# A subtraction of the causal convolution moved from VectorE to GpSimd, in the first and the last batch element

## The chip, the core and the metric

The kernel runs on one core of a Trainium2 chip. The core has a matrix engine (TensorE, PE in the profile), a vector engine (VectorE, DVE), a scalar engine (ScalarE, ACT), a general engine (GpSimd, POOL) and a queue engine that issues most of the loads (SyncE, SP). They work side by side and wait for each other on semaphores. The metric is the time of one execution on the device in microseconds (us); lower is better.

## What is computed

The input `x` is (4, 512, 128, 64): four batch elements `b`, T = 512 time steps, and D = 128*64 = 8192 features. Two layers follow one another. The part that matters here is in layer 0, after the attention and the convolution over frequency:

```python
x = x + fo                                            # called x2 in the kernel
xn = layernorm(x.reshape(b, t, d), ln_time_g, ln_time_b)
xt = jnp.swapaxes(xn, 1, 2)
to = lax.conv_general_dilated(xt, time_W, (1,), [(KS - 1, 0)],
                              dimension_numbers=('NCH', 'OIH', 'NCH'), feature_group_count=d)
to = to + time_b[None, :, None]
to = layernorm(jnp.swapaxes(to, 1, 2), time_ln_g, time_ln_b)
x = x + to.reshape(b, t, f, h)
mid = jax.nn.gelu(x @ ffn_W1 + ffn_b1)
x = x + (mid @ ffn_W2 + ffn_b2)
```

The layernorm takes, for each batch element and time step, the mean and the variance over all 8192 features. The convolution has three taps along time, a set of its own for every feature (`KS` = 3), and looks only back. Layer 1 then adds a moving average over time to a filter in the frequency domain (Fourier transform, a matrix product per frequency and channel, inverse transform).

## The kernel before

Layer 0 holds its data with features on the 128 partitions and time along the row. D is cut into `NCH` = 64 chunks of 128 features, and the chunks are handled in `NPR` = 32 pairs; a tile of a pair is 128 partitions x 2 x 512 float32, which the profile writes as 128x1024. For each batch element there are six stages, written as Python generators: `project` and `scan` (attention's projections and its recurrence), `attend_and_convolve` (the attention's output, the frequency convolution, and `x2`, stored to DRAM), `convolve_time` (the causal convolution), `open_feed` and `feed_forward`. A planner, `in_turn`, interleaves two stages at a time, by shares written out by hand. The pairs of stages around the change are `convolve_time(0)` beside `attend_and_convolve(1)`, and `convolve_time(3)` beside `feed_forward(2)`. What the planner sets by hand is TensorE's order alone; the order on the other engines is made by the language's scheduler when the kernel is built, except where an instruction is told to keep the order of the program.

`convolve_time(b)` makes the causal convolution of all 32 pairs. For b = 1 and b = 2, 14 of the 32 (`AHEAD`) are made earlier, in `convolve_ahead`, which runs inside the `feed_forward` of the element before; for b = 0 and b = 3 (`B - 1`) all 32 are made in `convolve_time`. For each pair, `normed` loads `x2` from DRAM on the SP queue (L643), multiplies it by 1/std (`rb`, L644), and subtracts mean/std (`mb`, L647). `rb` and `mb` are rows over time, the same on all partitions, and are read for both chunks of the pair (`pair_of`). All inputs and outputs of L644 and L647 are in SBUF, as float32, and L647 works in place.

`tapped` then makes the convolution, for each of the two chunks: ScalarE multiplies by the last tap and adds the bias (L652), and VectorE adds the other two taps, each a multiply and an add on a shifted row (L656). GpSimd then corrects the first two time steps of both chunks (L662, 128x4 elements) and issues the store of the result (L663). ScalarE makes the square of the result (L703), and TensorE sums the result and its square over the features two steps later (`add_up`, L252), for the second layernorm.

For b = 0 the normed tile has two buffers (`kd`) and the result three (`k3`, named `to`); for b = 3 they are three (`x1`, named `x`) and four (`z`).

In the loop beside `convolve_time(0)`, VectorE also makes, for each pair of b = 1: the sum of attention's output and `x` (L542, its first input in PSUM), its product with 1/std (L546, both inputs in SBUF), and `x2` (L596, its first input in PSUM). GpSimd issues the store of that `x2` (L599). Beside `convolve_time(3)`, VectorE makes, for each pair of b = 2: a product and a difference for the second layernorm (L724 and L725, SBUF), a sum (L736, SBUF), and the two sums that end the feed-forward (L793, first input in PSUM). GpSimd issues the store of every second pair's output (L810).

Only `normed` is edited; it is called from `convolve_ahead` and `convolve_time`.

Of the kernel before, what the change touches and what calls it, by code (L numbers as in the profile page):

```python
# [12 lines left out]
ALU = mybir.AluOpType  # L13
# [67 lines left out]
def layer0(ctx, tc, dram, x, xt, vecs, wkvr, wo, wdec, wconv, fbias, w1, fb1, w2, fb2, x4):  # L81
# [4 lines left out]
    nc = tc.nc  # L86
    B = x.shape[0]
# [202 lines left out]
    def pair_of(row):  # L290
        return row.unsqueeze(1).to_broadcast([P, 2, SL])
# [349 lines left out]
    def normed(b, i, x2, xr, rb, mb, pinned=False):  # L641

        nc.sync.dma_start(x2, x2d[b][2 * i : 2 * i + 2].rearrange("c p t -> p c t"))  # L643
        first = nc.vector.tensor_tensor(xr, x2, pair_of(rb), ALU.mult)  # L644
        if pinned:
            tc.keep_in_program_order(first)
        nc.vector.tensor_tensor(xr, xr, pair_of(mb), ALU.subtract)  # L647

    def tapped(b, i, xr, to, pinned=False):
        for j in range(2):  # L650
# [14 lines left out]
    def convolve_ahead(b, bank):  # L665


        rb, mb = yield from rows(bank, *carried[b], "rm3")
        ahead[b] = rb, mb
        for i in range(AHEAD):  # L670
            xr = spare("x1", SL)
            normed(b, i, xr, xr, rb, mb, True)
            yield
            tapped(b, i, xr, spare("z", SL), True)
            yield

    def convolve_time(b):
# [10 lines left out]
        for k in range(n + 2):  # L688
            while waiting and waiting[0][0] == k - 2:
                add_up(st, 0, *waiting.pop(0)[1:], added == 0, added == NPR - 1)  # L690
                added += 1
            if k < n:
                if b == B - 1:

                    x2, xr, to, sq = spare("xp", SL), spare("x1", SL), spare("z", SL), two(bk, "sq")
                else:
                    x2 = bk.tile([P, 2, SL], F32, tag="kx", name="x2", bufs=3)
                    xr, to = two(bk, "kd"), bk.tile([P, 2, SL], F32, tag="k3", name="to", bufs=3)
                    sq = bk.tile([P, 2, SL], F32, tag="sq4", name="sq4", bufs=2)

                normed(b, made + k, x2, xr, rb, mb, made > 0 and k < 4)
                tapped(b, made + k, xr, to)
                nc.scalar.activation(sq, to, AF.Square)  # L703
                waiting.append((k, to, sq))
                i = k * made // n
                if i != (k + 1) * made // n:

                    to = fetch("kh", tod, b, i)
                    sq = bk.tile([P, 2, SL], F32, tag="mid", name="sq5", bufs=4)
                    nc.scalar.activation(sq, to, AF.Square)  # L710
                    waiting.append((k, to, sq))
            yield 7.0 * (NPR + 2) / (n + 2)
# [532 lines left out]
```

## Time and profile before

| what | value |
|---|---|
| median of 3 runs | 3669.21 us (3665.94 to 3675.53) |
| the profiled execution | 3668.25 us, of which the span of the profile is 3666.5 us |
| clock granted to TensorE, mean over the span | 0.985 |
| L644 and L647 for b = 0 | 32 each, 520 to 767 us from the span's start |
| L644 and L647 for b = 3 | 32 each, 2086 to 2355 us |
| VectorE: L644, L647 | 1.22 us each, 128x1024 |
| VectorE: L656 | 0.74 us each, 128x511 or 128x510 |
| GpSimd: L662 | 128x4, from 0.19 to 8.04 us |

A row of the profile has the line of the kernel, the engine, the operation, the tiles (output<-inputs), the shapes, how often it runs, its busy time and the mean of one. Neighbouring VectorE operations overlap by a few hundredths of a microsecond in the records, so the distance between their starts is a little less than the duration that is shown. The waits view has one line for each pair of a waiting line and the line that it waited for: the sum in us, how many times, and the longest. A duration on GpSimd includes the time in which the operation has been started and waits for SBUF.

### The profile page before, as it was taken

Reading aid. Unit: us, or ns where it says so; the run is one execution under the profiler, and the core shown is the slowest. Engines: PE = TensorE matmul, PEld = TensorE weight load, DVE = VectorE, ACT = ScalarE, POOL = GpSimd, SP = SyncE. Lnnn points to the kernel's source line nnn. Section 1 sums busy time; section 2 is a strip of 40 time slices with the busy share of each in tenths; the row PEclk is TensorE's granted clock in tenths of the full one; section 3 lists DMA queues with packets and bytes.
Section 4 is the critical chain, followed back from the end, with each engine's and each line's share of the span. In section 5 each row is a group of like instructions: output and inputs, shape, how many; then the busy total and the mean of one; then the engine's idle time right before and its main releaser. Section 6 shows DMA issues by size and latency. Waiting matters only on the chain. (4 is left out here: it accounts for less than half of the span.)

```text
span 3666.5 us, 53980 instructions
## 1 busy us (share of the span) xinstructions
PE 3458.3 (94%) x20297; PEld 1363.8 (37%) x20297; DVE 2707.6 (74%) x3530; ACT 1787.3 (49%) x2363; POOL 448.6 (12%) x657
## 2 busy tenths in 40 slices
PE   8989998889998899999899989999999999999998
PEld 3433332234333223433322333343334833328433
DVE  4476779976776996677699799956677277892677
ACT  0013445655666565666656688878864200252100
POOL 0000012210111211010122121100001000001000
PEclk9999999999999999999999999999999999999999
DMA  9876657787885788788478678646668478994688
GB/s 314 288 260 232 225 187 257 257 280 269 288 275 174 265 275 289 271 282 282 164 264 284 214 255 266 227 169 213 233 197 266 149 254 289 300 302 148 224 281 263
DMA packets 427732, 910.48 MB, mean 248 GB/s; under 512 B 32848, under 2 KB 83664, under 8 KB 423376
## 3 DMA queue, kind: packets, MB, share of 16 engines
q1 hardware_dynamic: 353904, 637.11, 53.3%
q0 software_dynamic: 71680, 268.46, 20.3%
q8 instruction: 162, 2.65, 0.3%
q10 hardware_dynamic: 1888, 1.45, 0.1%
q14 instruction: 98, 0.80, 0.1%
HBM read 638.39 MB, written 268.50 MB: 247 GB/s over the span
## 5 line engine op out<-in xcount | busy, mean ns | idle before, releaser
L780 PE MATMUL p<-mid,w_sb 64*64 64x512 f32 x2048 | 551.5, 596 | 17.6 <-DVE wx L793 17.6
L780 PE MATMUL pb<-mid,w_sb 64*64 64x512 f32 x2048 | 534.0, 596 | 0.0
L770 ACT ACTIVATE mid<-c,fb_sb 128x1024 f32<-128x1024 f32 x256 | 284.3, 1111 | 93.0 <-PE c L765 90.8
L770 ACT ACTIVATE mid<-m,fb_sb 128x1024 f32<-128x1024 f32 x256 | 284.6, 1112 | 92.0 <-PE m L765 90.8
L765 PE MATMUL c<-x,w_sb 64*64 64x512 f32 x2016 | 279.0, 606 | 12.8 <-ACT mid L770 6.5
L765 PE MATMUL m<-x,w_sb 64*64 64x512 f32 x2016 | 283.0, 613 | 7.4 <-ACT ob L814 5.0
L780 PEld LDWEIGHTS p<-mid,w_sb 64*64 64x64 f32 x2048 | 154.1, 134 | 291.9 <-issue 262.1
L1091 ACT COPY two<-a 128x512 f32<-128x512 f32 x64 | 37.5, 585 | 432.0 <-PE a L1086 432.0
L414 PE MATMUL a<-xp,wx 128*128 128x512 f32 x512 | 235.2, 603 | 0.5 <-DVE me L269 0.5
L1114 PE MATMUL b<-xin,avg_sb 128*128 128x512 f32 x512 | 230.8, 593 | 3.3 <-DVE xin L1120 3.3
L1120 DVE TENSOR_TENSOR xin<-b,pm 128x512 f32<-128x512 f32 x256 | 159.1, 683 | 101.3 <-PE b L1117 86.3
L601 ACT ACTIVATE sq<-x 128x1024 f32<-128x1024 f32 x128 | 135.0, 1055 | 156.9 <-DVE x L596 156.8
L252 PE MATMUL st<-x,ones 128*32 128x512 f32 x512 | 185.2, 611 | 24.5 <-DVE x L596 24.5
L656 DVE SCALAR_TENSOR_TENSOR to<-kd,vec,to 128x511 f32<-128x511 f32 (+1 forms) x272 | 196.9, 742 | 10.4 <-ACT to L652 8.1
L733 ACT ACTIVATE kd<-kd,vec 128x512 f32<-128x512 f32 x256 | 192.7, 803 | 3.1 <-DVE kd L725 3.1
L966 DVE COPY xf<-b 128x256 f32<-128x256 f32 x128 | 54.3, 424 | 179.0 <-PE b L1060 170.0
L542 DVE TENSOR_TENSOR x<-a,xp 128x1024 f32<-128x1024 f32 x128 | 156.0, 1219 | 38.2 <-PE a L538 35.6
L656 DVE SCALAR_TENSOR_TENSOR z<-x,vec,z 128x511 f32<-128x511 f32 x240 | 175.6, 744 | 5.0 <-ACT z L652 3.6
L736 DVE TENSOR_TENSOR x<-kd,kx 128x1024 f32<-128x1024 f32 x126 | 154.0, 1222 | 33.4 <-ACT kd L733 33.4
L538 PE MATMUL a<-rst,wo_sb 64*64 64x512 f32 x1024 | 143.3, 627 | 27.5 <-DVE x L542 25.2
L793 DVE SCALAR_TENSOR_TENSOR x4t<-p,fb_sb,x 128x512 f32<-128x512 f32 x64 | 47.7, 746 | 160.0 <-PE pb L780 157.6
L724 DVE TENSOR_TENSOR kd<-kh,rm 128x1024 f32<-128x1024 f32 x128 | 155.6, 1219 | 7.1 <-ACT rm L286 4.6
(275 smaller groups left out, 6773.5 us busy)
## 6 DMA issues: line engine op xcount, KB each, us to landing
xp<-in_xt SPq DMA_DIRECT2D x256, 512.0 KB
kh<-to SPq DMA_DIRECT2D x156, 512.0 KB
x<-x POOLq DMA_DIRECT2D x128, 512.0 KB, 4.4
kx<-x SPq DMA_DIRECT2D x128, 512.0 KB
x<-ob POOLq DMA_DIRECT2D x64, 1024.0 KB, 8.1
xin<-x SPq DMA_DIRECT2D x64, 1024.0 KB
out<-xin POOLq DMA_DIRECT2D x64, 1024.0 KB, 6.3
x<-x SPq DMA_DIRECT2D x96, 512.0 KB
```

Source lines behind the costliest of these rows:

```text
L252: nc.tensor.matmul(st[32 * q : 32 * q + 32, :], lhsT=ones, rhs=src[:, j, :], start=first, stop=last,)
L414: nc.tensor.matmul(pa[:, k, :], lhsT=wq[:, j, k * P : (k + 1) * P], rhs=xp[:, j, :], start=first and j == 0, stop=last and j == 1,)
L542: nc.vector.tensor_tensor(x1, at, xp, ALU.add)
L656: tap = nc.vector.scalar_tensor_tensor(to[:, j, k:], xr[:, j, : SL - k], vec[:, w, c], to[:, j, k:], ALU.mult, ALU.add)
L724: nc.vector.tensor_tensor(d, to, pair_of(rb), ALU.mult)
L733: tc.keep_in_program_order(nc.scalar.activation(d[:, j, :], d[:, j, :], AF.Identity, bias=vec[:, B4, c], scale=vec[:, G4, c]))
L736: nc.vector.tensor_tensor(x3, d, x2, ALU.add)
L765: nc.tensor.matmul(pm[halves[j], h, :], lhsT=w1_sb[halves[h], q * H : (q + 1) * H], rhs=x3[halves[h], j, :], start=True, stop=True,)
L770: gelu = nc.scalar.activation(mid, pm, AF.Gelu_apprx_tanh, bias=fb1_sb[:, q : q + 1])
L780: nc.tensor.matmul(sums2[i][j][halves[h], :], lhsT=w2_sb[halves[j], q, :], rhs=mid[halves[j], h, :], start=q == 0, stop=q == 3,)
L1114: nc.tensor.matmul(po[j], lhsT=avg_sb[:, j, :], rhs=xin[:, j, :], start=True, stop=False)
L1120: nc.vector.tensor_tensor(by_n(xin[:, j, :]), by_n(po[j]), by_c(pm[j % 2][:, j // 2, :]), ALU.add)
```

## The change

One line of `normed` changes. The subtraction of mean/std is issued on GpSimd where `b` is 0 or 3; for b = 1 and b = 2 it stays on VectorE. The product with 1/std before it and the taps after it stay where they were.

```diff
         first = nc.vector.tensor_tensor(xr, x2, pair_of(rb), ALU.mult)
         if pinned:
             tc.keep_in_program_order(first)
-        nc.vector.tensor_tensor(xr, xr, pair_of(mb), ALU.subtract)
+        (nc.gpsimd if b in (0, B - 1) else nc.vector).tensor_tensor(xr, xr, pair_of(mb), ALU.subtract)
```

So 64 instructions, 32 in each of the two loops, go from VectorE's queue to GpSimd's. When the kernel is built, the scheduler also orders the other instructions of these two loops on VectorE, ScalarE and SP somewhat differently, since it places the moved instructions anew; TensorE's order stays as it was, and so do the shapes and the number of all instructions and transfers.

## The prediction

> **What bounds the kernel now.** I read the page's busy line first, then the windows around the two loops that the change touches (for batch elements 0 and 3, `b` = 0 and `b` = 3), then the groups and waits inside them. Over the whole span the bound is TensorE:
>
> ```profile
> PE 3458.3 (94%) x20297; PEld 1363.8 (37%) x20297; DVE 2707.6 (74%) x3530; ACT 1787.3 (49%) x2363; POOL 448.6 (12%) x657
> ```
>
> That is an average. In the windows view (PE, PEld, DVE, ACT, POOL busy us, then clock, DMA share, GB/s) the two loops look different:
>
> ```profile
> 508.00:766.00 258.00, 230.86 (x1310) 62.74 (x1309) 251.65 (x274) 154.80 (x212) 68.35 (x91) 0.99 0.76 256
> 2124.00:2355.00 231.00, 211.53 (x1740) 78.35 (x1733) 228.89 (x258) 199.28 (x237) 45.50 (x62) 0.97 0.77 256
> ```
>
> In the first, the causal convolution of b=0 beside attend_and_convolve of b=1, VectorE is busy 251.7 of 258 us. In the second, the convolution of b=3 beside feed_forward of b=2, 228.9 of 231. VectorE sets the pace there, and the waits from 400 to 1000 us and from 2000 to 2450 us agree that TensorE is the one that waits:
>
> ```profile
> PEld st L252 <- DVE x L596: 43.3, 29, 4.6
> PEld a L538 <- DVE x L542: 30.5, 24, 2.2
> PEld p L780 <- DVE wx L793: 25.5, 13, 6.5
> ```
>
> So one microsecond saved or lost on VectorE in these loops is about one microsecond of the kernel, until TensorE binds.
>
> **What is removed.** 32 subtractions (L647) leave VectorE in each loop. One shows as 1.22 us, but three in a row take 3.50 us, so the pitch is (3.50-1.22)/2 = 1.14 us, as neighbours overlap by 0.08. Five taps (L656) in a row take 3.39 us: pitch (3.39-0.74)/4 = 0.66. Removed: 32 x 1.14 = 36.5 us in each loop, 73 us in all. If nothing came back, TensorE's own busy time would stop the gain first: 258-231 = 27 us in the first loop. In the second, 2092 to 2355 us, TensorE is busy 22.7 + 211.5 = 234 of 263 us, so 29. The most that can be won is 56 us.
>
> **What is added.** 64 subtractions on GpSimd, on 128x1024 elements with two SBUF inputs. No row has this, so I bound one from below and above. Of the nearest rows, clearing 128x128 takes 209 ns against 102 for 128x4: 0.86 ns an element. The one-input operation takes 405 ns for 256 elements (L1053) against 228 for 4 (L233): 0.70 an element, though it reads and writes. So one pass costs about 0.8 ns an element, on 0.2 us of fixed time (the 4-element L662 has a minimum of 0.19). With both reads and the write overlapped: 0.2+0.8 = 1.0 us. Reads in turn: 0.2+1.6 = 1.85. All three in turn: 2.65. The two-input 4-element row is too short to choose. I take 2.25, midway between the last two, as I expect the reads not to overlap and do not know of the write.
>
> **What it collides with.** Here is the part that decides. These are lines of the timeline (start, length):
>
> ```profile
> 598.88 1.22 DVE L644 TENSOR_TENSOR kd<-x,rm 128x1024 f32<-128x1024 f32 x1
> 599.11 1.05 POOL L662 TENSOR_TENSOR to<-to,vec 128x4 f32<-128x4 f32 x1 [0.20 <-issue]
> 600.02 1.22 DVE L596 TENSOR_TENSOR x<-c,x 128x1024 f32<-128x1024 f32 x1
> ...
> 608.33 1.22 DVE L596 TENSOR_TENSOR x<-m,x 128x1024 f32<-128x1024 f32 x1
> 608.56 0.19 POOL L662 TENSOR_TENSOR to<-to,vec 128x4 f32<-128x4 f32 x1 [5.40 <-issue]
> ...
> 2107.79 8.04 POOL L662 TENSOR_TENSOR z<-z,vec 128x4 f32<-128x4 f32 x1 [0.23 <-DVE z L656]
> ```
>
> The same four-element GpSimd operation takes 0.19 us beside L596, whose first input is in PSUM, and 1.05 us beside L644, which has both inputs in SBUF: it ends 0.06 us after L644 does (598.88+1.22 = 600.10, and 599.11+1.05 = 600.16). At 2107.79 it waits 8 us, through eight such VectorE operations back to back, and ends as L793, with a PSUM input, starts. The two engines do not read SBUF side by side when VectorE reads two tensors there. What a long GpSimd read does to VectorE, no row shows: four elements are over too soon. From below VectorE loses nothing, from above it stands for all of GpSimd's time that its own PSUM operations do not cover. I take the upper end, since a port that cannot be shared in one direction is unlikely to be shared in the other.
>
> [...]
>
> **The sum.** The built order gives what VectorE issues next after each L644, and GpSimd's L647 waits for that L644. With L644's end as zero: GpSimd begins at 0.145 (as L662 does after a tap), and ends at 0.145 + H. VectorE's next operation starts at -0.08.
> - First loop, 30 of 32 tiles: next is L596 or L542 (PSUM, 1.14), which runs undisturbed. The operation after it should start at 1.06 and starts when GpSimd ends: loss H + 0.145 - 1.06 = H - 0.92. Against 1.14 saved: H - 2.06, which is +0.19 at 2.25.
> - Second loop, 21 of 32: next are two L793 (PSUM, 2 x 0.66): loss H + 0.145 - 1.24, net H - 2.24, which is +0.01.
> - The other 2 and 11: next is L644, L724, L725 or L656, two SBUF inputs, no cover: net H + 0.145 + 0.08 - 1.14 = H - 0.92, which is +1.33.
>
> First loop 30 x 0.19 + 2 x 1.33 = 8.4 us; second 21 x 0.01 + 11 x 1.33 = 14.8; 23 us in all. With H of 1.85 the same sum is -4.4 + 3.3 = -1; with 2.65 it is 21.2 + 27.6 = +49.
>
> The queue behind the new instruction: on GpSimd come the store of x2 (L599, 0.73 us to issue), the fix of the first two steps (L662), the store of its result (L663, 0.72) and in the second loop the store of x4 (L810). Per tile that is 2.25 + 0.73 + up to 1.05 + 0.72 and about a microsecond of waits, some 6 us, against 258/32 = 8.1 us for a tile, so the queue keeps up and stands ready at each L644. Who waits for it: ScalarE's square (L703, now 17.8 us for L662 in all), then TensorE's sums two steps later; a delay of 2 us is inside these two steps. TensorE's order is the same. SP's loads in both loops are issued in a somewhat altered order, with the same transfers; I cost this at nothing, as the windows show a DMA share of 0.76 and no row of VectorE waits for a load there. If that cover went, one load late by its own issue of 0.4 us in each of 64 tiles would be 26 us. What is not covered is the opening of each loop, where taps wait for a first tile: 1.3 us longer in the first, and three in line in the second, some 3 x 1.1 = 3.3 us, less what VectorE does meanwhile. I add 2 us. Total +25 us.
>
> The profiled execution took 3668.25 us (span 3666.5 and 1.75 around it); 3668.25 + 25 = 3693. The median of the three runs is 3669.21, 1 us above, so I leave it at 3693.
>
> **The rivals.**
> 1. VectorE is truly relieved: GpSimd and VectorE alternate at a finer grain, or VectorE's operations go on during GpSimd's. For it: four-element operations delay no VectorE operation visibly. Against: the 8 us wait. Then TensorE binds, at best 3668 - 56 = 3612; as engines in turn wait for each other some half of it is likelier, about 3635. Faster. It decides if VectorE pays less than about 0.9 us for one GpSimd subtraction.
> 2. It comes out even: H near 1.85, so the loss equals what is saved: 3667.
> 3. GpSimd is starved, as at 2107.79, whenever it misses the PSUM operation. The 11 uncovered tiles of the second loop would each finish about 6 us late, and if the taps wait for that, 11 x 6 = 66 us: 3734. Against it: three xr buffers let taps run two tiles behind.
>
> **How the numbers follow.** Forecast 0.53, rival 1 0.24, rival 2 0.18, rival 3 0.05. 0.3% of 3669 is 11 us, about what a measurement of this kernel tells from no change. So slower 0.58, same 0.18, faster 0.24. The low end must take in half of rival 1: 3636. The high end is H = 2.65: 3668 + 49 + 2 = 3719, say 3720. Since cases of both signs carry weight: the forecast's own range is 3680 to 3720.
>
> **What would show it.** Right: L647 on POOL at 2.2 us or more; L656 or L736 stretched from 0.74 and 1.22 us when it follows the PSUM operation, VectorE still busy over 95% in both loops, the first loop longer by some 8 us and the second by 15. Wrong: L656 at 0.74 us throughout and VectorE at about 85%, with the loops shorter; or L647 below 1.9 us. If the loops keep their length but the kernel moves, the reordered loads did it.

## The result, and the profile after

The changed kernel takes 3686.88 us (median of 8 runs, 3678.25 to 3700.57) against 3666.57 us (8 runs, 3659.32 to 3677.37) before: a ratio of 1.0055, 95% interval 1.0042 to 1.0069. It is slower by 0.42 to 0.69%, some 20 us. The profiled execution has a span of 3695.1 us, 28.6 more than the one of before; it is one of the slower ones of its eight.

First the busy line of the changed kernel's page:

```profile
PE 3459.8 (94%) x20297; PEld 1370.5 (37%) x20297; DVE 2710.6 (73%) x3466; ACT 1788.5 (48%) x2363; POOL 605.1 (16%) x721
```

VectorE (DVE) runs 64 instructions fewer and is busy 2710.6 us, 3 us more than before. So the time that the 64 subtractions took is still on VectorE, in other rows. GpSimd (POOL) is busy 156 us longer. The rows of two single lines of code, the subtraction and the taps, show where VectorE's time went (columns: shortest, median and longest in ns, first and last start):

```profile
L647 POOL TENSOR_TENSOR kd<-kd,rm x32: 2347/2360/3322, 524.7 to 777.1; 128x1024 f32<-128x1024 f32 x32
L647 POOL TENSOR_TENSOR x<-x,rm x32: 2345/2363/3349, 2115.2 to 2385.3; 128x1024 f32<-128x1024 f32 x32
```

```profile
L656 DVE SCALAR_TENSOR_TENSOR to<-kd,vec,to x272: 733/744/3276, 528.9 to 2051.2; 128x511 f32<-128x511 f32 x123, 128x510 f32<-128x510 f32 x13
L656 DVE SCALAR_TENSOR_TENSOR z<-x,vec,z x240: 683/743/4271, 889.3 to 2409.9; 128x511 f32<-128x511 f32 x111, 128x510 f32<-128x510 f32 x9
```

The rows of the taps before:

```profile
L656 DVE SCALAR_TENSOR_TENSOR to<-kd,vec,to x272: 729/742/753, 527.1 to 2028.9; 128x511 f32<-128x511 f32 x119, 128x510 f32<-128x510 f32 x17
L656 DVE SCALAR_TENSOR_TENSOR z<-x,vec,z x240: 676/744/790, 871.7 to 2380.5; 128x511 f32<-128x511 f32 x112, 128x510 f32<-128x510 f32 x8
```

The subtraction takes 2.36 us on GpSimd. The taps (L656) have the same median as before, 0.74 us, but the longest went from 0.79 to 4.27. One period of the first loop in the timeline of VectorE, and of GpSimd, shows how (start, length):

```profile
669.38 1.23 DVE L644 TENSOR_TENSOR kd<-x,rm 128x1024 f32<-128x1024 f32 x1
670.52 1.22 DVE L596 TENSOR_TENSOR x<-m,x 128x1024 f32<-128x1024 f32 x1
671.66 2.73 DVE L656 SCALAR_TENSOR_TENSOR to<-kd,vec,to 128x511 f32<-128x511 f32 x2
674.31 1.22 DVE L542 TENSOR_TENSOR x<-a,xp 128x1024 f32<-128x1024 f32 x1
...
678.01 1.23 DVE L644 TENSOR_TENSOR kd<-x,rm 128x1024 f32<-128x1024 f32 x1
```

```profile
670.70 2.36 POOL L647 TENSOR_TENSOR kd<-kd,rm 128x1024 f32<-128x1024 f32 x1
```

A period of the same loop before, on VectorE:

```profile
749.38 1.22 DVE L644 TENSOR_TENSOR kd<-x,rm 128x1024 f32<-128x1024 f32 x1
750.64 1.22 DVE L647 TENSOR_TENSOR kd<-kd,rm 128x1024 f32<-128x1024 f32 x1
751.79 1.22 DVE L596 TENSOR_TENSOR x<-m,x 128x1024 f32<-128x1024 f32 x1
...
756.50 1.53 DVE L656 SCALAR_TENSOR_TENSOR to<-kd,vec,to 128x511 f32<-128x511 f32 x2
758.07 1.23 DVE L644 TENSOR_TENSOR kd<-x,rm 128x1024 f32<-128x1024 f32 x1
```

L596, with an input in PSUM, keeps its 1.22 us under GpSimd's operation. The first of the two taps after it starts at 671.66 and ends only after GpSimd has, which is at 673.06: the pair takes 2.73 us where two taps took 1.40 to 1.53 before. One period is 678.01 - 669.38 = 8.63 us; before, the L644 at 749.38 and 758.07 were 8.69 apart. In the middle of the loop the change is nearly even: 1.2 to 1.3 us of stall in place of 1.14 of subtraction.

I take as stretch what an operation on VectorE lasts beyond the median of its form while L647 runs on GpSimd. It sums to 37.8 us in the first loop and 34.7 in the second, with a median per tile of 1.21 and 1.07 us. The 32 subtractions that were taken away are worth 36.5 us in each loop. So the stalls eat what the relief gives, and little more.

The two windows that follow lie between the same two matmuls of each loop, before and then after (columns as in the windows of the prediction, VectorE the third busy time):

```profile
504.70:809.40 304.70, 271.18 (x1510) 78.91 (x1506) 281.46 (x324) 174.69 (x238) 75.82 (x102) 0.99 0.77 260
2069.90:2385.20 315.30, 280.07 (x2254) 107.41 (x2249) 300.04 (x340) 260.79 (x308) 67.85 (x80) 0.95 0.72 242
```

```profile
505.50:826.90 321.40, 265.76 (x1510) 83.69 (x1506) 285.72 (x292) 175.16 (x238) 155.30 (x134) 0.96 0.75 246
2092.20:2414.70 322.50, 284.74 (x2254) 108.23 (x2249) 297.77 (x308) 261.28 (x308) 146.69 (x112) 0.94 0.72 237
```

Both together are 23.9 us longer. VectorE is busy 2.0 us longer in them and idle 21.9 us longer. So with the stalls set against the relief, the loss in this trace is time in which VectorE has nothing to run.

Where that is, TensorE shows. Its order is the same in both kernels, so the start of the same matmul can be compared. How much later it starts after the change:

```
place (us, trace of before)   504.7   549.5   747.9   809.4   2069.9   2121.9   2187.6   2385.2   end
late by (us)                    0.8     7.5    12.1    17.5     22.3     32.1     28.1     29.5    28.6
```

Of the first loop's 16.7 us, 6.7 come in its opening, 4.6 in the 200 us of its middle, and 5.4 at its end. The second loop loses 9.8 in its opening, wins 4.0 back and loses 1.4 more. Between the loops, where the instructions are the same, the traces drift by 4.8; I do not count that to the change, since the kernel with only the first loop changed (below) drifts by -0.7 there. The opening of the second loop on VectorE and on GpSimd:

```profile
2112.51 1.22 DVE L644 TENSOR_TENSOR x<-xp,rm 128x1024 f32<-128x1024 f32 x1
2118.42 8.03 DVE L656 SCALAR_TENSOR_TENSOR z<-x,vec,z 128x511 f32<-128x511 f32 x7 [4.69 <-ACT z L652]
...
2134.40 3.48 DVE L644 TENSOR_TENSOR x<-xp,rm 128x1024 f32<-128x1024 f32 x3
2142.22 6.25 DVE L656 SCALAR_TENSOR_TENSOR z<-x,vec,z 128x511 f32<-128x511 f32 x4 [4.34 <-ACT z L652]
```

```profile
2115.17 7.42 POOL L647 TENSOR_TENSOR x<-x,rm 128x1024 f32<-128x1024 f32 x3 [10.73 <-ACT rm L286]
...
2133.31 4.63 POOL L662 TENSOR_TENSOR z<-z,vec 128x4 f32<-128x4 f32 x1 [1.36 <-DVE z L656]
2138.24 0.72 POOL L663 DMA_DIRECT2D to<-z  x1 [0.30 <-POOL z L662]
2138.99 6.95 POOL L647 TENSOR_TENSOR x<-x,rm 128x1024 f32<-128x1024 f32 x3
```

Three subtractions stand in a row on GpSimd, 7 us, where VectorE did three in 3.5. VectorE has nothing else to do and is idle for 4.69 and 4.34 us, until ScalarE (L652) has the first tile; before, it was idle here once, for 1.40 us. Then the taps collide with the next subtraction. The second three also start late: the first of the three L644 ends at 2135.62, but the four-element L662 stands ahead in GpSimd's queue and takes 4.63 us beside VectorE's taps and L644, and then the store L663 is issued. So the first subtraction begins at 2138.99, 3.4 us after its input was there.

### The profile page after: what moved, and what is told of

Read it like the earlier page. It is cut to its first block, busy times and chain, and to the rows that moved or that the text cites. A ratio compares the mean times of both kernels' runs of the same rounds, so it can differ in the third digit from the quotient of the medians.

```text
span 3695.1 us, 53995 instructions
## 1 busy us (share of the span) xinstructions
PE 3459.8 (94%) x20297; PEld 1370.5 (37%) x20297; DVE 2710.6 (73%) x3466; ACT 1788.5 (48%) x2363; POOL 605.1 (16%) x721
## 3 DMA queue, kind: packets, MB, share of 16 engines
q8 instruction: 162, 2.65, 0.3%
## 5 line engine op out<-in xcount | busy, mean ns | idle before, releaser
L656 DVE SCALAR_TENSOR_TENSOR to<-kd,vec,to 128x511 f32<-128x511 f32 (+1 forms) x272 | 233.7, 873 | 18.0 <-ACT to L652 13.2
L656 DVE SCALAR_TENSOR_TENSOR z<-x,vec,z 128x511 f32<-128x511 f32 (+1 forms) x240 | 190.3, 806 | 14.1 <-ACT z L652 12.6
L736 DVE TENSOR_TENSOR x<-kd,kx 128x1024 f32<-128x1024 f32 x126 | 171.7, 1363 | 35.0 <-ACT kd L733 35.0
L252 PE MATMUL st<-x,ones 128*32 128x512 f32 x512 | 169.2, 608 | 17.5 <-DVE x L596 17.5
L599 POOL DMA_DIRECT2D x<-x x128 | 93.5, 730 | 483.4 <-DVE x L596 459.2
L793 DVE SCALAR_TENSOR_TENSOR x4t<-p,fb_sb,x 128x512 f32<-128x512 f32 x64 | 47.7, 745 | 159.5 <-PE pb L780 157.0
```

Source lines behind the costliest of these rows:

```text
L252: nc.tensor.matmul(st[32 * q : 32 * q + 32, :], lhsT=ones, rhs=src[:, j, :], start=first, stop=last,)
L656: tap = nc.vector.scalar_tensor_tensor(to[:, j, k:], xr[:, j, : SL - k], vec[:, w, c], to[:, j, k:], ALU.mult, ALU.add)
L736: nc.vector.tensor_tensor(x3, d, x2, ALU.add)
```

## The experiments

All are edits of the one line of `normed`, in the kernel before (one run adds a tile besides). A `+` line stands in place of that line, and `(...)` in it stands for the arguments of the subtraction as it was. Differences in us are worked out from the ratio and 3670 us. TensorE's order is the same in all of them. Theory A: VectorE's operations with two SBUF inputs stand still while GpSimd reads SBUF. Theory B: GpSimd is only a slow link of the chain and a full queue. What is given as "loop I" and "loop II" is how much later the same matmul starts over 504.7 to 809.4 us, or over 2069.9 to 2385.2, in the one trace of that kernel against the one of before (for a loop that a run leaves as it was, it came to 3.5 and 0.0).

**The subtraction left out**

```diff
-nc.vector.tensor_tensor(xr, xr, pair_of(mb), ALU.subtract)
+b in (0, B - 1) or nc.vector.tensor_tensor(xr, xr, pair_of(mb), ALU.subtract)
```

> The subtraction of mean/std is left out for b = 0 and b = 3 (the result of these two lacks it); b = 1 and b = 2 keep it on VectorE. It shows how much VectorE's relief is worth with nothing put in its place. Both theories: faster than before. VectorE loses 2 x 36.5 us; TensorE's own busy time allows 56 us at most; I expect about half to three quarters, 3668 - 30 to 40 = 3628 to 3638. If it is less than 10 us faster, VectorE did not set the pace of the loops, and the theory of the prediction falls at its first step.

Measured: 3623.49 against 3674.86 us, ratio 0.9871 (0.9850 to 0.9891), 47 us less; loop I -31, loop II -15. So VectorE does set the pace, and its relief alone is worth close to the 56 us that TensorE's busy time allowed, more than I expected.

**GpSimd writes, but reads nothing**

```diff
+[nc.gpsimd.memset(xr, v) for v in (1.0, 0.5)] if b in (0, B - 1) else nc.vector.tensor_tensor(...)
```

> In place of the subtraction for b = 0 and b = 3, GpSimd fills the same tile with a constant, twice (the result of these two is not the reference's). This occupies GpSimd for about 2 us at the same place of the same chain, but it reads nothing from SBUF. Theory A (VectorE stands still for the reads of GpSimd): no stretched L656 and L736, loops as short as with the subtraction left out, within 12 us of that run. Theory B (what costs is that GpSimd is a slow link of the chain, in time and in its queue): as slow as the changed kernel, 3680 to 3690.

Measured: 3627.10 against 3674.86, ratio 0.9876 (0.9848 to 0.9903), the same as with the subtraction left out; loop I -25, loop II -21. The rows of this kernel's L647 and L656:

```profile
L647 POOL MEMSET kd<- x64: 946/952/974, 515.1 to 731.1; 128x1024 f32 x64
```

```profile
L656 DVE SCALAR_TENSOR_TENSOR to<-kd,vec,to x272: 732/744/753, 518.9 to 1998.5; 128x511 f32<-128x511 f32 x121, 128x510 f32<-128x510 f32 x15
```

Two fills are 1.9 us at the same place of the same chain. No tap is stretched (longest 0.753 us here and 0.787 in the second loop's row, where it was 0.790 before), and no fill waits (0.942 to 0.978 in both loops). Theory B would have had this kernel at 3680 to 3690; it falls. An occupied GpSimd costs nothing here. Its reads do. For the openings the run says less: the fills do not read mean/std, so they need not wait for that row (L286) as the first subtractions do, and two of them are 0.4 us shorter than one subtraction.

**GpSimd's subtraction added, nothing taken away**

```diff
+free_s, scrap = [True], rowp.tile([P, 2, SL], mybir.dt.bfloat16, tag="scrap", name="scrap")
...
 nc.vector.tensor_tensor(xr, xr, pair_of(mb), ALU.subtract)
+b in (0, B - 1) and nc.gpsimd.tensor_tensor(scrap, xr, pair_of(mb), ALU.subtract)
```

> VectorE keeps all its subtractions, and GpSimd makes the same subtraction once more for b = 0 and b = 3, into a tile that nobody reads (bfloat16, for space). So GpSimd's reads are added and nothing is taken from VectorE or put on the chain. Theory A: each of the 64 costs VectorE 1.2 to 2.3 us, depending on what stands after it in VectorE's queue; 75 to 130 us slower than before, 3745 to 3800. Theory B: nobody waits for the result, so under 12 us slower, 3667 to 3680.

Measured: 3760.29 against 3674.86, ratio 1.0242 (1.0215 to 1.0269), 89 us more; loop I +48, loop II +42. Nobody waits for the result, so theory B does not explain it: 89 / 64 = 1.4 us a subtraction. The stretch on VectorE adds up to 46.4 and 43.5 us, with a median per tile of 1.26 and 1.07, as in the changed kernel. The sum, 89.9 us, is all that the kernel lost. The rows of the added subtraction:

```profile
L647 POOL TENSOR_TENSOR scrap<-kd,rm x32: 2342/2376/3280, 526.7 to 813.5; 128x1024 bf16<-128x1024 f32 x32
L647 POOL TENSOR_TENSOR scrap<-x,rm x32: 2338/2358/3274, 2143.1 to 2447.1; 128x1024 bf16<-128x1024 f32 x32
```

**The first three pairs stay on VectorE**

```diff
+(nc.gpsimd if b in (0, B - 1) and i > 2 else nc.vector).tensor_tensor(xr, xr, pair_of(mb), ALU.subtract)
```

> As the change, but the first three pairs of each loop keep the subtraction on VectorE. In the profile of the changed kernel TensorE falls behind by 6 us in the opening of the first loop and by 10 in that of the second, and by little in between. If the opening carries the loss (pairs in a row with nothing to cover them, and taps that wait): 10 to 15 us less than the changed kernel, 3672 to 3677. If the loss is even over the tiles: 58/64 of it, within 3 us of the changed kernel, 3684 to 3687.

Measured: 3683.15 against 3674.86, ratio 1.0028 (1.0015 to 1.0040), between the two expectations. Loop I +10.6 (16.7 with the change), loop II +3.5 (7.2). In the trace the opening of the first loop is repaired (0.2 us late at 549.5, not 7.5), and that of the second is not: it still loses 6.1 us between 2069.9 and 2121.9. There L662 again takes 4.63 us (at 2117.52), three subtractions follow in a row (at 2123.19, 6.95 us), and VectorE is again idle for 4.34. Loss is left in the first loop after the opening, so the opening carries part of it, not all.

**One loop at a time**

```diff
+(nc.gpsimd if b == 0 else nc.vector).tensor_tensor(xr, xr, pair_of(mb), ALU.subtract)
```

> Only the first loop's subtraction (b = 0) goes to GpSimd. The prediction gave it 8.4 us of tiles and 1.3 of the opening, so 3676 to 3680; the changed kernel's trace has TensorE 17.5 us late after this loop, of which some 5 came at its end while TensorE's clock was halved. If that is part of the change and not chance, 12 to 18 us slower than before; if it is chance, 6 to 12.

```diff
+(nc.gpsimd if b == B - 1 else nc.vector).tensor_tensor(xr, xr, pair_of(mb), ALU.subtract)
```

> Only the second loop's subtraction (b = 3) goes to GpSimd. The prediction gave it 14.8 us of tiles and up to 3.3 of the opening; in the changed kernel's trace TensorE loses 10 us in its opening, wins 4 back, and nothing after. So by the trace 5 to 9 us slower than before, by the prediction 15 to 18. If the two loops do not influence each other, this and the run with b = 0 alone add to the change's 20 us, within 6.

Measured against 3673.50: 3686.26 for b = 0, ratio 1.0036 (1.0023 to 1.0048), and 3679.42 for b = 3, ratio 1.0016 (1.0002 to 1.0029). Together 0.52%, where the change has 0.55: the two loops add. The first costs 13 us, more than the 9.7 that I had given it, and the second 6, less than 15 to 18. By what I had written down, 13 us speaks for the end of the first loop as a part of the change (12 to 18) and not as chance (6 to 12). But it lies close to the bound, and the interval, 0.23 to 0.48%, is 8 to 18 us. In the trace of b = 0 alone the matmuls are again 7.6 us late in the opening; at the end of the loop the lateness grows by 1.7 us, not by 5.4. In that of b = 3 alone, whose first loop is as before, it grows there by 2.6. So I take most of the 5.4 for chance; it is not shown.

**GpSimd takes one chunk of the pair, or a third of the time steps**

```diff
+[e.tensor_tensor(xr[:, j, :], xr[:, j, :], mb, ALU.subtract) for e, j in ((nc.gpsimd, 1), (nc.vector, 0))]
+    if b in (0, B - 1) and i > 2 else nc.vector.tensor_tensor(xr, xr, pair_of(mb), ALU.subtract)
```

> GpSimd subtracts one chunk of each pair (128x512), VectorE the other; the first three pairs of each loop stay on VectorE. If GpSimd's reads are free while VectorE works on a PSUM input, the operation, about 0.2 + 1.08 = 1.28 us long, nearly fits into L596 (1.14) and into the two L793 (1.32): VectorE saves 0.54 us a tile, stands 0.2 in the first loop and 0 in the second, and pays 0.7 more than it saves at the 14 tiles without cover: 26 x -0.34, 18 x -0.54, 14 x 0.7, together -9 us, 3658 to 3668. If cover is of no importance and only the length of GpSimd's operation counts: half of the run with the opening left on VectorE, 3 to 8 us slower than before.

```diff
+[e.tensor_tensor(xr[:, :, s], xr[:, :, s], pair_of(mb)[:, :, s], ALU.subtract)
+    for e, s in ((nc.gpsimd, slice(0, 170)), (nc.vector, slice(170, SL)))] if b in (0, B - 1) and i > 2 else ...
```

> As the run with one chunk, but GpSimd takes the first 170 of 512 time steps of both chunks (128x340), VectorE the rest. The operation should be 0.2 + 0.72 = 0.9 us and fit wholly into the PSUM operations: 0.35 us saved a tile, nothing lost at 44 tiles, 0.45 lost at 14: -9 us, about as the half. If cover is of no importance: no gain, within 5 us of before.

Measured against 3673.50: half 3661.19, ratio 0.9971 (0.9961 to 0.9982), 11 us faster than before; third 3667.19, ratio 0.9980 (0.9967 to 0.9992), 7 us. Both beat the kernel before; between the two there is no certain difference. It is the same engine, the same operation and the same place, but cut to the length of its cover, and with the openings left to VectorE. A period of the half in the second loop, VectorE and GpSimd:

```profile
2247.19 0.69 DVE L647 TENSOR_TENSOR x<-x,rm 128x512 f32<-128x512 f32 x1
2247.80 0.74 DVE L793 SCALAR_TENSOR_TENSOR wx<-p,fb_sb,x 128x512 f32<-128x512 f32 x1
2248.46 0.74 DVE L793 SCALAR_TENSOR_TENSOR wx<-pb,fb_sb,x 128x512 f32<-128x512 f32 x1
2249.12 1.22 DVE L736 TENSOR_TENSOR x<-kd,kx 128x1024 f32<-128x1024 f32 x1
```

```profile
2247.24 1.77 POOL L647 TENSOR_TENSOR x<-x,rm 128x512 f32<-128x512 f32 x1
```

GpSimd's operation waits for VectorE's own L647 to end at 2247.88 and then runs beside the two L793, which have an input in PSUM. It ends at 2249.01, and L736 starts at 2249.12, with its plain 1.22 us. Alone the operation takes 1.26 us (its shortest). The stretch on VectorE sums to 8.1 us for 58 tiles, against 72.5 for 64 in the changed kernel.

**The half in the loops of b = 1 and 2 as well**

The edit is shown against the run with one chunk.

```diff
-    if b in (0, B - 1) and i > 2 else ...
+    if not pinned and i > 2 else ...
```

> The split of a pair between GpSimd and VectorE, as in the run with one chunk, now also in the loops of b = 1 and b = 2, for the pairs that are not held to the program's order (28 more tiles; VectorE makes the same L542 and L596 beside them). If the cover by PSUM operations is what makes it pay, 28 x 0.34 = 9 us less than the run with one chunk, where these loops are paced by VectorE: 3650 to 3658. If VectorE does not set the pace there: the same as that run, 3658 to 3664.

Measured: 3659.30 against 3673.60, ratio 0.9959 (0.9943 to 0.9975), 15 us faster than before. Beside 0.9971 for the half alone that is no certain difference; whether the further 28 tiles bring anything stays open. Of the kernels that leave nothing out it has the lowest ratio.

**GpSimd reads one input only**

```diff
+[nc.gpsimd.tensor_scalar(xr, xr, v, 0.0, ALU.mult, ALU.add) for v in (0.5, 2.0)]
+    if b in (0, B - 1) else nc.vector.tensor_tensor(...)
```

> In place of the subtraction for b = 0 and b = 3, GpSimd multiplies the tile by 0.5 and then by 2 (the subtraction of mean/std is left out there): two operations with one SBUF input, each about 0.2 + 0.7 = 0.9 to 1.0 us, so the pair is as long as the two fills. If one read stream is enough to stop VectorE's operations with two SBUF inputs, they stand about 0.9 us a tile after their cover: 3645 to 3670, with stretched L656 and L736. If only GpSimd's second stream collides: as with the two fills, 3620 to 3635, and nothing stretched.

Measured: 3655.59 against 3673.60, ratio 0.9952 (0.9935 to 0.9969), inside the range for "one stream is enough". The rows of its L647 and L656:

```profile
L647 POOL TENSOR_SCALAR kd<-kd x64: 1037/1060/3073, 519.4 to 760.1; 128x1024 f32<-128x1024 f32 x64
```

```profile
L656 DVE SCALAR_TENSOR_TENSOR to<-kd,vec,to x272: 731/744/2018, 525.3 to 2026.9; 128x511 f32<-128x511 f32 x121, 128x510 f32<-128x510 f32 x15
```

The pair of operations is as long as the two fills, 2 x 1.04 us, but taps stretch to 2.02 us, and the stretch sums to 48.3 us; with the fills it was nothing. Of the 47 us that the relief is worth, 18 are left.

## Why the prediction was right, step by step

**VectorE sets the pace in the two loops: shown.** The subtraction left out gives 47 us, of 56 that TensorE allowed.

**The collision, with VectorE paying for GpSimd's whole operation: shown.** This was the step that no row of before showed, since its four-element operations were too short; I took it as an estimate from the 8.04 us that GpSimd had waited for VectorE. The fills, the added subtraction and the one-input operation settle it for this kernel: reads of GpSimd held up operations of VectorE with two SBUF inputs, and writes did not. In the row of the first loop the longest tap was 0.753 us under the fills, 2.02 under the one-input reads, 2.86 under the added subtraction. The "port" of the prediction is my picture of it; the runs show which engine stands still, and for how long, and not what the two share. Rival 1 (VectorE truly relieved, 3635) needed VectorE to lose less than 0.9 us for each; it lost 1.07 to 1.21.

**The length H: 2.36 us for the 2.25 that I took** between 1.85 and 2.65. Rival 2 (H near 1.85, even) is out. (Its sum was also wrong: 21 x -0.39 + 11 x 0.93 is +2.0, not +3.3, so -2.4 in all; nothing else rests on it.) The shortest here was 2.345.

**Tiles with cover: right, near nothing.** I had +0.19 us a tile in the first loop and +0.01 in the second; with stretches of 1.21 and 1.07 for 1.14 saved it is +0.07 and -0.07. The tap does not lose quite as much as the sum had it: a stretched L656 ends 0.55 us after GpSimd, not 0.74.

**Tiles without cover: mis-sized.** I charged 1.33 us for each of 13, 17 us in all. Where two L644 stand in a row in the second loop, GpSimd's first operation waits for the second L644 and then has its cover after all, and only the next one has none: in four such pairs 2.06 - 1.22 = 0.84 and 2.84 - 0.74 = 2.10 us, 2.94 for 2.28 saved, 0.33 a tile.

**The tiles as a whole: 23 us predicted, about nothing measured.** The stretch of all 64, those of the openings included, is 72.5 us against 73 saved, and VectorE's busy time in the two loops grew by 2.0. With the H that came, my sum would even have been 30. So the stall alone makes the change even, not slower, and the forecast's main term was far too large.

**The opening: mis-sized the other way.** I gave both openings 2 us. They cost 6.7 and 9.8 in the trace, of which the second loop wins 4.0 back; VectorE is idle 5.2 and 7.7 us longer there. What I missed is that VectorE has nothing else to run: it waits for 2.4 us a tile on GpSimd in series, in the second loop twice for three tiles, the second time behind a starved L662.

The errors in the tiles and in the openings have opposite signs, and the total, +25 us predicted, stands beside +20 by the medians. That it came out so near is chance; what was right is that VectorE pays for GpSimd's reads, so that the relief is worth nothing. The split shows it too: I expected some 8 us from the first loop and 15 from the second, and the runs with one loop at a time have 13 and 6. And VectorE did not stay busy for over 95%: in the windows above its share fell from 92 to 89% and from 95 to 92%.

**Rival 3 (GpSimd starved for 6 us in uncovered tiles): not in the subtraction, but once ahead of it.** The longest subtraction took 3.35 us, one VectorE operation longer than the shortest. The 8 us wait of before has its like in the one L662 of 4.63, which held up the second three subtractions of the second opening by 3.4 us. What that alone cost was not tried.

**The order of SP's loads: no cost of its own is seen.** With the fills, SP's issues stand nearly in the order of the changed kernel (in the traces 2 of 1887 are out of place, against 52 between the changed kernel and the one before), and that kernel is 45 us faster than before.

## What to carry to other kernels

Before moving an elementwise operation from VectorE to GpSimd, look at what VectorE will issue while GpSimd reads. Where that had two inputs in SBUF, VectorE stood still here, and a relief of 1.14 us bought a median stall of 1.21 us a tile in the first loop and 1.07 in the second: about GpSimd's 2.36 us less the PSUM work that covered it. So cut the part for GpSimd to the length of the PSUM operations that follow (here 128x512 beside 1.2 to 1.3 us of them), and leave the first tiles of a loop, where nothing covers, on VectorE (1.22 us for the subtraction, against 2.36 on GpSimd; with three pairs this mended the opening of the first loop here, not that of the second). Ask as well what stands ahead of the moved operation in GpSimd's queue. An average busy share of 12% on GpSimd says nothing of this.

## What was not expected of the hardware

Operations of GpSimd back to back kept VectorE out as well, as those of VectorE had kept GpSimd out for 8.04 us before. Of the four taps that take 6.25 us at 2142.22, the first takes 4.27: it came while the second of three subtractions ran (2138.99 to 2145.94), did not get in between it and the third, and ended 0.55 us after that.

TensorE's granted clock fell at one place without a cause that I can name. At the end of the first loop it waited 4.2 us for L596, where it had waited 3.7, and the window around it (columns as in the windows of before) has a clock of 0.79 (0.51 from 784 to 796):

```profile
780.00:820.00 40.00, 33.43 (x110) 14.28 (x103) 17.61 (x38) 11.24 (x17) 6.28 (x10) 0.79 0.75 255
```

In the trace of before the window there shows

```profile
760.00:800.00 40.00, 32.90 (x146) 12.92 (x139) 24.29 (x45) 15.33 (x22) 8.76 (x13) 0.96 0.86 292
```

By the two numbers, 0.04 x 40 = 1.6 us of the clock were withheld before and 0.21 x 40 = 8.4 after, for half a microsecond more of waiting. Between the matmuls at 747.9 and 809.4 TensorE is busy 52.9 us before and 58.3 after, so the 5.4 us lost at this place are slower matmuls. Waiting longer does not explain it: the kernel with b = 0 alone waits 4.7 us for L596 there, has a clock of 0.92 between these matmuls (0.97 before, 0.85 after) and loses only 1.7. The kernel with the fills, where nothing collides, has 0.87. So I count it as chance of one execution and not as a cost of the change; no run here was made to settle it.
